# Another order of the score products in a cross-attention layer, with one mask moved ahead of one addition

## The chip, the cores and the metric

The kernel runs on one core of one Trainium2 chip, in one launch. The time is the device time of that core in microseconds (us); a kernel is run several times and the median counts. Five engines work side by side: PE multiplies matrices (its weight loads are listed apart as PEld), DVE is VectorE, ACT is ScalarE, POOL is GpSimd, and SP issues most of the transfers.

## The reference

One cross-attention layer with a feed-forward part, over 128 sequences of 128 tokens of width 256, 16 heads of 16 columns, hidden width 1024, all in float32:

```python
q = (query @ Wq + bq).reshape(b, s, N_HEADS, D_K).transpose(0, 2, 1, 3)
k = (key @ Wk + bk).reshape(b, s, N_HEADS, D_K).transpose(0, 2, 1, 3)
v = (values @ Wv + bv).reshape(b, s, N_HEADS, D_K).transpose(0, 2, 1, 3)
scores = jnp.einsum('bhqd,bhkd->bhqk', q, k) / jnp.sqrt(jnp.float32(D_K))
allowed = j < i + mask                      # mask = 0
scores = jnp.where(allowed, scores, NEG_INF)
attn = jax.nn.softmax(scores, axis=-1)
attn = attn.at[:, :, 0, :].set(0.0)
ctx = jnp.einsum('bhqk,bhkd->bhqd', attn, v)
attn_out = ctx.transpose(0, 2, 1, 3).reshape(b, s, d) @ Wo + bo
x = layer_norm(query + attn_out, ln1_g, ln1_b)
ffn = jax.nn.relu(x @ W1 + b1) @ W2 + b2
out = layer_norm(x + ffn, ln2_g, ln2_b)
```

`query` is `x`; `key` and `values` are both the context input. A query attends only to keys that stand before it.

## The kernel before

The 128 sequences are worked through as 64 pairs. The pairs run through a software pipeline: one step of it does the scores of pair p, the attention output of pair p-2, the first feed-forward product of pair p-3, the second of p-4, the projections of p+1, and so on. What each engine does, and in which order, is written out by hand: `ORDER` is a list of names, `step(p)`, for p from 9 to 60, calls the operation behind each name in turn, and every engine executes its own instructions in the order in which they were recorded. Pairs 7, 8, 61 and 62 use the same names, called one by one in lists of their own; the first seven pairs and the last are written out by hand. Semaphore waits between engines are put in by the framework where two operations touch the same data or the same bank.

PE's results go to eight banks, of 512 float32 numbers per partition. The operations around the change share them so:

- `weigh` (L586, L596) multiplies the attention weights of pair p-2 with its values; its result lies in bank 7.
- `context` (L614, two instructions on DVE) reads bank 7 and scales it by the softmax sums.
- `scores` (`scores_both`, L440) makes the scores of pair p. Its products use only 32 rows and 64 columns of the array, so that the array serves as eight tiles: four strips of 32 rows (r = 0 to 3) by the two sequences of the pair (s = 0, 1). The "high" half, queries 64 to 127, needs all 128 keys and takes products of 256 columns (two heads); its results lie in bank r. The "low" half, queries 0 to 63, can only see the first 64 keys and takes products of 128 columns; its results lie in bank 4+r. Each tile makes two low and two high products (m = 0 and 1). Strips 0 and 1 are called `one`, strips 2 and 3 `two`. So the low products of `two` write banks 6 and 7, and those of strip 3 write the bank that `context` reads.
- `maskA0`, `maskA1` (L464, DVE) add the mask to the low scores of strips 0 and 1 out of banks 4 and 5; `maskB` (L456) does so for strips 2 and 3, banks 6 and 7. `add3` (L1562) adds the mask to the high scores of strip 3 in bank 3, and `max3` (L1568) takes their maxima.
- `v1` (L1153, the values of pair p, bank 4) is the first work on PE behind the scores. `o1` (bank 5) and `q1` (bank 7) follow. These are products on the full array.

In the trace each float32 product shows as two records, a weight load and a matmul each; a score block of 32 products has 64.

Of the kernel before, what the change touches and what calls it, by code (L numbers as in the profile page):

```python
# [19 lines left out]
def tile_cross_attention_block(  # L20
# [83 lines left out]
    def weight(w, name):  # L104
        n = w.shape[0] // P
        t = const.tile([P, n, w.shape[1]], F32, tag=name, name=name)
        nc.sync.dma_start(t, w.rearrange("(k p) n -> p k n", p=P))
        return t
# [24 lines left out]
    wk = const.tile([P, KC, D], F32, tag="wk", name="wk")  # L133
# [29 lines left out]
    w1 = weight(W1, "w1")  # L163
# [3 lines left out]
    w2 = weight(W2, "w2")  # L167
# [18 lines left out]
    one = const.tile([1, P], F32, tag="one", name="one")  # L186
# [61 lines left out]
    def at_bank(i, name):  # L248
        return banks[:, i]
# [141 lines left out]
    def room(p, hi):  # L391

        st = states[p]
        if "sm" not in st:
            st["sm"] = wide(f"sm_{p}") if p != 1 else turned_all
        at = H * P if not hi else 0
        n = P if hi else HP
        st["sm", hi] = st["sm"][:, at : at + H * n].rearrange("p (h j) -> p h j", j=n)
        st["nmx", hi] = small.tile([P, H], F32, tag=f"nmx{hi}", name=f"nmx{hi}_{p}")
# [22 lines left out]
    def scores_both(p):  # L422

        st = states[p]
        st["both"] = True
        for hi in range(2):
            st["sps", hi] = [
                at_bank(r if hi else 4 + r, f"pss{hi}_{p}_{r}") for r in range(NS)
            ]
            room(p, hi)  # L430
        one, two = (0, 1), (2, 3)
        for strips, hi, m in (
            (one, 0, 0), (two, 1, 0), (one, 0, 1), (two, 1, 1),
            (one, 1, 0), (one, 1, 1), (two, 0, 0), (two, 0, 1),
        ):
            n = P if hi else HP
            for s in range(2):
                for r in strips:
                    strip, first = slice(32 * r, 32 * r + 32), s * P
                    nc.tensor.matmul(  # L440
                        st["sps", hi][r][
                            s * HP : (s + 1) * HP, m * 2 * n : (m + 1) * 2 * n
                        ].rearrange("p (e j) -> p e j", e=2),
                        st["qT"][strip, m, first + hi * HP : first + hi * HP + HP],
                        st["kT"][strip, m, :, first : first + n],
                        start=True, stop=True,
                    )
# [1200 lines left out]
    def bring_part(p, n):  # L1648
# [3 lines left out]
    OPS = {  # L1652
        "weigh": lambda p: weigh(p - 2),
        "scores": lambda p: scores_both(p),
        "context": lambda p: context(p - 2, True),
        "deviations": lambda p: scales_of(p),
# [96 lines left out]
    for n in range(3):  # L1753
        OPS[f"turn{n}"] = lambda p, n=n: turn(p, n < 2, n % 2)

    ORDER = """
        weigh addbo re0-2 vr-1 hf-2 re2-2 re1-2 turnx-1 xc2-1 re3-2 context scores res0 ro3-2
        ro0-2 br1 maskA0 ro2-2 add3 oc0 ro1-2 v1 maskA1 oc2 maskB hs0-1 o1 max3 vk1 vk0 q1
        lowmax eh7 oc1 v2 br0 xs2-1 qk w1-1 hs1-1 ok eh6 tokc-1 w2-1 tokx vk2 el3 oc3 hs3-1 v3
        add1 el4 w5-1 max1 br3 el0 add2 o2 cc0 wk-1 eh3 k1 finish1-1 vb ok2 va eh2 q2 stats2 o3  # L1760
        cc2 kk w6-1 max2 cc1 el6 add0 hs2-1 br2 h1-1 vf el2 ob oa max0 w3-1 qk2 cc3 eh5 xs0-1
        q3 eh0 xs1-1 o4 wk2-1 k2 qa finish2-1 qb hk-1 w7-1 or stats1 kk2 eh4 k3 xc0 means h6-1
        load-1 store-1 eh1 wb-1 xs3-1 ka xc1 wa-1 el5 q4 kb h5-1 xc3 turn1 el1 deviations
        w4-1 hk2-1 turn0 el7 k4 h7-1 res1 hk5-1 turn2 kr h2-1 vs-1 ks ha-1 qr h3-1 ks2 loadx norm2
        hb-1 h4-1 recip norm1 wr-1 turni v4
    """.split()

    EMPTY = {'w1': 5, 'h1': 4, 'w2': 5, 'h2': 4, 'w3': 5, 'h3': 5, 'w4': 4, 'h4': 5, 'w5': 4, 'h5': 5, 'w6': 4, 'h6': 5, 'w7': 5, 'h7': 4, 'v1': 3, 'o1': 1, 'q1': 2, 'k1': 2, 'v2': 3, 'o2': 2, 'q2': 2, 'k2': 3, 'v3': 2, 'o3': 2, 'q3': 3, 'k3': 2, 'v4': 2, 'o4': 2, 'q4': 3, 'k4': 2}
# [269 lines left out]
    tokens(5, "c")  # L2038
    bring(3, nc.sync, LATE_FIRST[7:])
    scores_both(4)  # L2040
    mask(4, 0, A)
    mask(4, 1, A)
# [31 lines left out]
    spread_values(4)  # L2074
    stack_values(4)
    scores_both(5)
    tokens(6, "c")
    mask_high(5, 2, 2)
# [1024 lines left out]
```

## Time and profile before

| what | value |
|---|---|
| median of 3 runs | 1464.37 us (1463.9 to 1467.12) |
| the profiled execution | 1463.95 us |
| its span in the profile | 1462.1 us |
| busy: PE, PEld, DVE, ACT, POOL | 99%, 95%, 94%, 89%, 87% |
| granted clock of TensorE | 1.0 over the span |
| one step of the pipeline | 21.97 us |

The span runs from the first to the last instruction. Idle time of an engine is listed with what ended it. A timeline merges neighbouring instructions of one line into a row: the start, how long until the last of them ended, and their number; a row names only the first shape.

### The profile page before, as it was taken

What the parts mean: (1) busy time and instruction counts of PE and PEld (TensorE: products, weight loads), DVE (VectorE), ACT (ScalarE), POOL (GpSimd) and SP (SyncE); (2) the same over time, 40 slices, a digit from 0 to 9 for tenths busy, and PEclk for the clock granted to TensorE, in tenths of its full rate; (3) what the DMA queues carried; (4) which work ended last, traced back from release to release, by engine and by line L of the source; (5) the groups of instructions that cost most, each with busy time, mean ns of one, the idle gap of its engine ahead of it and who ended that gap; (6) DMA issues with size and microseconds to landing.
All of it is one profiled execution on the core that took longest, in us unless ns stands there. A gap on an engine that the chain in (4) does not pass through costs nothing.

```text
span 1462.1 us, 62019 instructions
## 1 busy us (share of the span) xinstructions
PE 1445.1 (99%) x20713; PEld 1389.5 (95%) x20713; DVE 1372.1 (94%) x3175; ACT 1302.0 (89%) x5559; POOL 1268.4 (87%) x1872
## 2 busy tenths in 40 slices
PE   9999899999999999999999999999999999999998
PEld 7788799999999999999999999999999999999998
DVE  6987999999999999999999999999999999999777
ACT  5659899999999999999999999999999999999763
POOL 5977898988988988988988988988988988988875
PEclk9999999999999999999999999999999999999999
DMA  8264766766766766766766766766766766765451
GB/s 206 70 143 105 178 158 150 161 160 154 161 160 152 162 158 155 161 159 154 161 155 158 161 155 158 162 162 149 164 154 157 164 152 157 166 158 127 117 131 51
DMA packets 367881, 220.34 MB, mean 151 GB/s; under 512 B 280032, under 2 KB 335584, under 8 KB 367584
## 3 DMA queue, kind: packets, MB, share of 16 engines
q1 hardware_dynamic: 365296, 214.27, 64.2%
q8 instruction: 187, 3.06, 1.0%
q10 hardware_dynamic: 2288, 2.11, 0.7%
q14 instruction: 110, 0.90, 0.2%
HBM read 55.06 MB, written 18.09 MB: 50 GB/s over the span
## 4 chain that ended last, share of the span: by engine, by line
PE 92%; DVE 3%; POOL 1%; ACT 1%; DMA 1%; issue 1%; SPq 0%; POOLq 0%; DVEq 0%; ACTq 0%
PE banks L1153 48%; PE banks L1364 24%; PE banks L440 6%; PE banks L596 4%; PE banks L586 2%; PE banks L875 1%; PE banks L1050 1%; PE banks L300 1%; PE banks L977 1%; ACT sm L937 1%; PE banks L635 1%; POOL sm L476 1%; DVE sm L464 1%; PE banks L1412 0%; PE banks L894 0%
## 5 line engine op out<-in xcount | busy, mean ns | idle before, releaser
L937 ACT ACTIVATE sm<-banks,nmx 128x128 f32<-128x128 f32 x944 | 338.9, 391 | 19.1 <-DVE nmx L1568 15.5
L937 ACT ACTIVATE sm<-sm,nmx 128x64 f32<-128x64 f32 x944 | 323.4, 378 | 0.3 <-DVE nmx L926 0.3
L533 DVE STREAM_TRANSPOSE turned<-sm 128x1024 f32<-128x1024 f32 x186 | 217.1, 1215 | 4.8 <-DMA brought<-turned 3.0
L937 ACT ACTIVATION_READ_ACCUMULATOR sm<-banks,nmx 128x1 f32 x944 | 218.9, 232 | 0.0
L937 ACT ACTIVATION_READ_ACCUMULATOR sm<-sm,nmx 128x1 f32 x944 | 216.4, 229 | 0.0
L1153 PE MATMUL banks<-wt,hS 128*128 128x128 f32 x1344 | 177.7, 275 | 0.0
L1364 PE MATMUL banks<-xS,w1t 128*128 128x128 f32 x1344 | 177.4, 275 | 0.0
L1153 PEld LDWEIGHTS banks<-wt,hS 128*128 128x128 f32 x1344 | 163.6, 192 | 0.1
L1364 PEld LDWEIGHTS banks<-xS,w1t 128*128 128x128 f32 x1344 | 163.5, 192 | 0.1
L1568 DVE TENSOR_REDUCE nmx<-banks 128x4 f32<-128x512 f32 x224 | 152.6, 681 | 1.9
L1557 POOL TENSOR_TENSOR hS<-hT 128x512 f32<-128x512 f32 x116 | 147.8, 1275 | 3.1 <-ACT hT L882 1.4
L1364 PE MATMUL banks<-brought,w 128*128 128x128 f32 x896 | 118.3, 275 | 0.0
L1153 PE MATMUL banks<-w,hT 128*128 128x128 f32 x896 | 109.7, 275 | 0.0
L1364 PEld LDWEIGHTS banks<-brought,w 128*128 128x128 f32 x896 | 109.0, 192 | 0.0
L1618 POOL TENSOR_TENSOR x1b<-x,g_r 128x512 f32<-128x512 f32 x56 | 72.4, 1292 | 39.6 <-ACT x L709 39.6
L1153 PEld LDWEIGHTS banks<-w,hT 128*128 128x128 f32 x896 | 104.8, 192 | 0.0
L440 PE MATMUL banks<-kT,qT 32*64 32x128 f32 (+1 forms) x3840 | 98.4, 331 | 1.8 <-ACT vz L1278 1.5
L1393 ACT ACTIVATE hT<-hT,b1e_c 128x256 f32<-128x256 f32 x224 | 95.6, 509 | 0.3 <-DVE hT L1389 0.2
L1562 DVE TENSOR_TENSOR banks<-banks,neg 128x256 f32<-128x256 f32 x224 | 93.4, 417 | 0.1
L440 PEld LDWEIGHTS banks<-kT,qT 32*64 32x64 f32 x3840 | 79.5, 131 | 12.6 <-ACT vz L1278 1.8
L1219 ACT ACTIVATE kr<-banks,b_c 128x128 f32<-128x128 f32 x224 | 81.8, 403 | 2.7 <-PE banks L1153 2.7
L764 POOL TENSOR_TENSOR t<-t,g_r 128x512 f32<-128x512 f32 x62 | 79.1, 1276 | 5.3 <-ACT t L746 3.9
(324 smaller groups left out, 4795.9 us busy)
## 6 DMA issues: line engine op xcount, KB each, us to landing
brought<-turned SPq DMA_DIRECT2D x936, 128.0 KB, 2.4
out_dram<-t SPq DMA_DIRECT2D x63, 256.0 KB, 4.0
xb<-in_x_dram SPq DMA_DIRECT2D x124, 128.0 KB, 3.3
cb<-in_ctx_dram SPq DMA_DIRECT2D x124, 128.0 KB, 3.3
x<-in_x_dram SPq DMA_DIRECT2D x56, 256.0 KB, 2.9
kT<-kr SPq DMA_DIRECT2D x112, 128.0 KB, 2.2
brought<-turned SPq DMA_DIRECT2D x40, 96.0 KB, 2.5
w<-in_L_xattn_W_dram SPq DMA_DIRECT2D x2, 1024.0 KB, 7.4
```

What stands on the lines that cost most here:

```text
L440: nc.tensor.matmul(st["sps", hi][r][s * HP : (s + 1) * HP, m * 2 * n : (m + 1) * 2 * n].rearrange("p (e j) -> p e j", e=2), st["qT"][strip ...
L533: nc.vector.transpose(turned[:, :, at : at + 256].rearrange("p j (n a) -> p n j a", a=32), states[p]["sm", hi].rearrange("p h j -> p (h j) ...
L764: nc.gpsimd.tensor_tensor(t2, t2, g2_r[:, None, :].to_broadcast([P, 2, D]), ALU.mult)
L937: nc.scalar.activation(sm[:, h, :], src, AF.Exp, bias=nmx[:, h : h + 1], scale=1.0, **({"accum_out": st["su"][:, at : at + 1]} if summed e ...
L1153: nc.tensor.matmul(out, left(k) if self.depth > 1 else left, right(k) if self.depth > 1 else right, start=(n == 1 and k == 0), stop=(k == ...
L1219: nc.scalar.activation(self.k[:, m, s * P : (s + 1) * P], src, AF.Identity, bias=bk_c[:, m : m + 1], scale=1.0,)
L1364: nc.tensor.matmul(ps[:, i * P : (i + 1) * P].rearrange("p (n a) -> p n a", a=32), left(i), right, start=(n in (1, 2, 5) and i == 0), stop ...
L1393: nc.scalar.activation(self.hT[:, f, at], self.hT[:, f, at] if src is None else src, AF.Relu, bias=b1e_c[:, f : f + 1], scale=1.0,)
L1557: engine.tensor_tensor(c[:, n], left, right, how)
L1562: nc.vector.tensor_tensor(ps[:, :, HP:], ps[:, :, HP:], neg[:, 1, None, :].to_broadcast([P, 4, HP]), ALU.add)
L1568: nc.vector.tensor_reduce(states[p]["nmx", 1][:, 4 * b : 4 * b + 4], banks[:, b].rearrange("p (n j) -> p n j", j=P), AX.X, ALU.max, negate ...
L1618: nc.gpsimd.tensor_tensor(st["x1b"], st["x1b"] if n else st["x1"], (be1b_r if n else g1_r)[:, None, :].to_broadcast([P, 2, D]), ALU.add if ...
```

## The change

The order of the eight groups of four products in `scores_both` is another one, and in `ORDER` the names `maskA1` and `add3` change places. The rest of the list is only wrapped in other places; no instruction is added, removed or resized.

```diff
         for strips, hi, m in (
-            (one, 0, 0), (two, 1, 0), (one, 0, 1), (two, 1, 1),
-            (one, 1, 0), (one, 1, 1), (two, 0, 0), (two, 0, 1),
+            (one, 0, 0), (two, 1, 0), (one, 0, 1), (one, 1, 0),
+            (two, 0, 0), (two, 0, 1), (one, 1, 1), (two, 1, 1),
         ):
...
     ORDER = """
...
-        ro0-2 br1 maskA0 ro2-2 add3 oc0 ro1-2 v1 maskA1 oc2 maskB hs0-1 o1 max3 vk1 vk0 q1
...
+        ro3-2 ro0-2 br1 maskA0 ro2-2 maskA1 oc0 ro1-2 v1 add3 oc2 maskB hs0-1 o1 max3 vk1
```

Each group is (strips, 1 for high and 0 for low, m), and holds four products: two strips by two sequences.

On PE, one step before (a score block and the first product of `v1`; `64x128` is a low product, `64x256` a high one; a row stands for one instruction or, with xN, for N like it; the names in brackets are the engines and transfer queues whose semaphores it waits for):

```order
L440 MATMUL banks<-kT_171,qT_12548 64x128 [waits DMAHW4_49,DMAHW3_49,Activation_49]
L440 MATMUL banks<-kT_171,qT_12548 64x128 x3
L440 MATMUL banks<-kT_171,qT_12548 64x256 [waits DVE_49]
L440 MATMUL banks<-kT_171,qT_12548 64x256 x3
L440 MATMUL banks<-kT_171,qT_12548 64x128 x4
L440 MATMUL banks<-kT_171,qT_12548 64x256 x4
L440 MATMUL banks<-kT_171,qT_12548 64x256 [waits Activation_49]
L440 MATMUL banks<-kT_171,qT_12548 64x256 x7
L440 MATMUL banks<-kT_171,qT_12548 64x128
L440 MATMUL banks<-kT_171,qT_12548 64x128 [waits DVE_49]
L440 MATMUL banks<-kT_171,qT_12548 64x128 x6
L1153 MATMUL banks<-wv,cT_12586 128x128 [waits DVE_49]
```

The same step with the change:

```order
L440 MATMUL banks<-kT_171,qT_12548 64x128 [waits DMAHW4_49,DMAHW3_49,Activation_49]
L440 MATMUL banks<-kT_171,qT_12548 64x128 x3
L440 MATMUL banks<-kT_171,qT_12548 64x256 [waits DVE_49]
L440 MATMUL banks<-kT_171,qT_12548 64x256 x3
L440 MATMUL banks<-kT_171,qT_12548 64x128 x4
L440 MATMUL banks<-kT_171,qT_12548 64x256 [waits Activation_49]
L440 MATMUL banks<-kT_171,qT_12548 64x256 x3
L440 MATMUL banks<-kT_171,qT_12548 64x128
L440 MATMUL banks<-kT_171,qT_12548 64x128 [waits DVE_49]
L440 MATMUL banks<-kT_171,qT_12548 64x128 x6
L440 MATMUL banks<-kT_171,qT_12548 64x256 x8
L1153 MATMUL banks<-wv,cT_12586 128x128 [waits DVE_49]
```

The low product that waits for DVE (the first of strip 3) stood behind all sixteen high products and is now behind eight of them; eight high products stand behind it.

On DVE, the same place before:

```order
L614 TENSOR_TENSOR cxT<-banks,brought 128x8x32 [waits PE_49]
L614 TENSOR_TENSOR cxT<-banks,brought 128x8x32
L464 TENSOR_TENSOR sm_13386<-banks,neg 128x256 [waits PE_49,Activation_49]
L1562 TENSOR_TENSOR banks<-banks,neg 128x4x64 [waits PE_49]
L464 TENSOR_TENSOR sm_13386<-banks,neg 128x256
L456 TENSOR_TENSOR sm_13386<-banks,neg 128x512 [waits PE_49]
```

And with the change:

```order
L614 TENSOR_TENSOR cxT<-banks,brought 128x8x32 [waits PE_49]
L614 TENSOR_TENSOR cxT<-banks,brought 128x8x32
L464 TENSOR_TENSOR sm_13386<-banks,neg 128x256 [waits PE_49,Activation_49]
L464 TENSOR_TENSOR sm_13386<-banks,neg 128x256 [waits PE_49]
L1562 TENSOR_TENSOR banks<-banks,neg 128x4x64 [waits PE_49]
L456 TENSOR_TENSOR sm_13386<-banks,neg 128x512
```

`context` and `maskA0` keep their places; the second L464 (`maskA1`) and L1562 (`add3`) have changed theirs, and the wait for PE ahead of `maskB` is now the one ahead of `add3`. ACT, POOL and SP have the same instructions in the same order as before.

More of the change, by code (lines that the diff above doesn't have):

```diff
@@ L1756, in tile_cross_attention_block @@
     ORDER = """
-        weigh addbo re0-2 vr-1 hf-2 re2-2 re1-2 turnx-1 xc2-1 re3-2 context scores res0 ro3-2
-        ro0-2 br1 maskA0 ro2-2 add3 oc0 ro1-2 v1 maskA1 oc2 maskB hs0-1 o1 max3 vk1 vk0 q1
[L1759 to L1765, printed above, removed]
+        weigh addbo re0-2 vr-1 hf-2 re2-2 re1-2 turnx-1 xc2-1 re3-2 context scores res0
+        ro3-2 ro0-2 br1 maskA0 ro2-2 maskA1 oc0 ro1-2 v1 add3 oc2 maskB hs0-1 o1 max3 vk1
+        vk0 q1 lowmax eh7 oc1 v2 br0 xs2-1 qk w1-1 hs1-1 ok eh6 tokc-1 w2-1 tokx vk2 el3 oc3
+        hs3-1 v3 add1 el4 w5-1 max1 br3 el0 add2 o2 cc0 wk-1 eh3 k1 finish1-1 vb ok2 va eh2
+        q2 stats2 o3 cc2 kk w6-1 max2 cc1 el6 add0 hs2-1 br2 h1-1 vf el2 ob oa max0 w3-1 qk2
+        cc3 eh5 xs0-1 q3 eh0 xs1-1 o4 wk2-1 k2 qa finish2-1 qb hk-1 w7-1 or stats1 kk2 eh4
+        k3 xc0 means h6-1 load-1 store-1 eh1 wb-1 xs3-1 ka xc1 wa-1 el5 q4 kb h5-1 xc3 turn1
+        el1 deviations w4-1 hk2-1 turn0 el7 k4 h7-1 res1 hk5-1 turn2 kr h2-1 vs-1 ks ha-1 qr
+        h3-1 ks2 loadx norm2 hb-1 h4-1 recip norm1 wr-1 turni v4
     """.split()
```

## The prediction

> **What bounds the kernel now.** I read the page's head and its chain of waits first, then one step of the pipeline, then the score blocks.
>
> ```profile
> span 1462.1 us, 62019 instructions
> PE 1445.1 (99%) x20713; PEld 1389.5 (95%) x20713; DVE 1372.1 (94%) x3175; ACT 1302.0 (89%) x5559; POOL 1268.4 (87%) x1872
> PE 92%; DVE 3%; POOL 1%; ACT 1%; DMA 1%; issue 1%; SPq 0%; POOLq 0%; DVEq 0%; ACTq 0%
> ```
>
> PE is the bound: it holds 92% of the chain. The waits that PE still shows in the pipeline are of one kind only (busy time by engine over one step, then waits by who waited, for whom, us in total, times, longest):
>
> ```profile
> 734.09:756.06 21.97, 21.97 (x335) 21.54 (x329) 21.30 (x52) 20.83 (x93) 19.66 (x30) 1.00 0.69 158
> PEld banks L1153 <- DVE sm L464: 9.1, 52, 0.3
> DVE t L1299 <- PE banks L1153: 31.4, 60, 1.3
> ```
>
> So a step lasts as long as PE's work, at full clock, and the one regular gap is ahead of `v1`, 52 times 0.17 us, put down to `maskA0`. DVE has 0.67 us of air in a step (21.97 - 21.30), and spends some 0.5 of it (31.4/60) waiting for PE at one place. Whatever lengthens the stretch from `weigh` to `v1` on PE therefore lengthens the step one to one. The timeline of that stretch, about pair 34:
>
> ```profile
> 733.53 0.63 PE L596 MATMUL banks<-brought,vz 128*32 128x64 f32 x32
> 733.57 0.70 DVE L1624 STREAM_TRANSPOSE turned<-x 128x512 f32<-128x512 f32 x1
> 734.09 1.61 PE L440 MATMUL banks<-kT,qT 32*64 32x128 f32 x64
> 734.23 0.76 DVE L614 TENSOR_TENSOR cxT<-banks,brought 128x256 f32<-128x256 f32 x2
> 734.97 0.42 DVE L464 TENSOR_TENSOR sm<-banks,neg 128x256 f32<-128x256 f32 x1
> 735.31 0.42 DVE L1562 TENSOR_TENSOR banks<-banks,neg 128x256 f32<-128x256 f32 x1
> 735.63 0.52 PEld L1153 LDWEIGHTS banks<-wv,cT 128*128 128x128 f32 x4 [0.17 <-DVE sm L464]
> 735.64 0.41 DVE L464 TENSOR_TENSOR sm<-banks,neg 128x256 f32<-128x256 f32 x1
> 735.97 0.68 DVE L456 TENSOR_TENSOR sm<-banks,neg 128x512 f32<-128x512 f32 x1
> 736.57 0.68 DVE L1568 TENSOR_REDUCE nmx<-banks 128x4 f32<-128x512 f32 x1
> 736.96 0.41 PEld L1153 LDWEIGHTS banks<-xT,wq 128*128 128x128 f32 x3
> ```
>
> `weigh` ends at 734.16; `context` starts 0.07 later, which is as soon as it can, and ends at 734.99. Counted from the start of the scores (734.09) that is +0.90. `v1` loads at +1.54. `maskA0` is over at 735.39, 0.24 ahead of `v1`, so I doubt the releaser that is named. Three blocks in which `context` ran late decide it (start of the scores, `context`, load of `v1`):
>
> ```profile
> 184.61 1.59 PEld L440 LDWEIGHTS banks<-kT,qT 32*64 32x64 f32 x64
> 185.02 0.71 DVE L614 TENSOR_TENSOR cxT<-banks,brought 128x256 f32<-128x256 f32 x2
> 186.38 0.52 PEld L1153 LDWEIGHTS banks<-wv,cT 128*128 128x128 f32 x4 [0.17 <-issue]
> ...
> 1173.51 1.40 PEld L440 LDWEIGHTS banks<-kT,qT 32*64 32x64 f32 x64
> 1173.71 0.72 DVE L614 TENSOR_TENSOR cxT<-banks,brought 128x256 f32<-128x256 f32 x2
> 1175.08 0.41 PEld L1153 LDWEIGHTS banks<-wv,cT 128*128 128x128 f32 x3 [0.17 <-issue]
> ...
> 1349.56 1.44 PEld L440 LDWEIGHTS banks<-kT,qT 32*64 32x64 f32 x64
> 1349.81 0.72 DVE L614 TENSOR_TENSOR cxT<-banks,brought 128x256 f32<-128x256 f32 x2
> 1351.17 0.52 PEld L1153 LDWEIGHTS banks<-wv,cT 128*128 128x128 f32 x4 [0.17 <-issue]
> ```
>
> The end of `context` lies at +1.12, +0.92 and +0.97 there, the load of `v1` at +1.77, +1.57 and +1.61. In all four blocks `v1` loads 0.64 to 0.65 us behind the end of `context`, whatever else varies. What hangs between them is the low products of strips `two`: strip 3 must not write bank 7 before `context` has read it. **The release of bank 7 by `context`, and what the array still has to do behind it, sets the start of `v1`.** At present that is four records per tile (two low products). The records of L440 that run in two narrow windows, with their shapes, show that the array is full up to that moment:
>
> ```profile
> L440 PE MATMUL banks<-kT,qT x16: 374/374/412, 734.6 to 735.0; 32*64 32x256 f32 x16
> ...
> L440 PE MATMUL banks<-kT,qT x15: 267/374/374, 734.8 to 735.1; 32*64 32x256 f32 x11, 32*64 32x128 f32 x4
> ```
>
> In 734.96 to 735.03 only high records run, on every tile; in 735.02 to 735.06 four low ones have started, just as `context` (734.99) lets them. The old order has its high products of `two` cover the wait for `context` almost exactly.
>
> **The change part by part.** Nothing is added or removed: the same 64 records, 54 score blocks from 184.61 to 1349.56 that follow a `context` directly. What a record costs its tile (groups by form; then a row of the timeline):
>
> ```profile
> L440 PE MATMUL banks<-kT,qT 32*64 32x256 f32 x1920 | 93.8, 383 | 0.3 <-ACT vd L379 0.3
> L440 PE MATMUL banks<-kT,qT 32*64 32x128 f32 x1920 | 80.9, 279 | 1.5 <-ACT vz L1278 1.5
> 724.48 1.06 PE L1153 MATMUL banks<-wt,hS 128*128 128x128 f32 x8
> ```
>
> Eight records of 128 columns take 1.06 us where one lasts 0.275: (1.06 - 0.275)/7 = 0.112 us of array each. One of 256 columns lasts 383 - 279 = 104 ns more: 0.216.
>
> *The low products of `two`, moved ahead.* Tiles `two` have, ahead of the wait, two high products now (4 x 0.216 = 0.86, from +0.03 to about +0.95 with the first load) and one with the change (0.43, to about +0.51). From +0.51 to +0.95 they stand still: bank 7 comes free no sooner, since `context` starts when `weigh` ends. Behind the waiting product PE's queue holds the rest of the block, the last high products of `one` and `two`; `one` still has its first high product to finish (to about +0.92) and loses little.
>
> *The high products, moved to the end.* Behind the release the tiles of `two` now do two low and one high product instead of two low ones: two records of 256 columns more, 2 x 0.216 = 0.43 us. `one` needs 0.43 behind the release and is done earlier. The gap from the end of `context` to `v1` grows from 0.64 to 1.07, the block from +1.54 to +1.97. Bounds: not under 0.40 (0.05 off, should the first low load be ready in time); not over 0.53 (strict order, below). I take 0.43, for these are the same records on the same tiles one behind the other.
>
> *`maskA1` ahead of `add3`.* `maskA1` comes 0.33 us earlier (735.31 for 735.64) and frees bank 5, for which nobody waits: nothing. `add3` needs the high products of strip 3, now the last of all. The scores end 0.07 behind `v1`'s load (734.09 + 1.61 = 735.70), so at about +2.04, `add3` starts 0.07 later at +2.11 instead of +1.22; between `maskA1` (over at about +1.6) and there DVE is idle for 0.5. `maskB` and `max3` behind it come at +2.44 and +3.04 (were +1.88 and +2.48): 0.56 later, against 0.43 on PE, thus 0.13 behind. Who waits for them: `q1` needs `maskB` out of bank 7. `maskB` would end at +3.12, `q1` loads at +2.87 + 0.43 = +3.30: 0.18 of room, with a wake of 0.07 still enough. The exponentials on ACT wait for `max3` and fall 0.13 behind too; ACT has 1.14 us of air in a step (21.97 - 20.83). DVE makes the 0.13 good where it waits 0.5 for PE. I cost this part at nothing; the cover that hides it is that 0.18, and if it is gone the step pays the difference, up to 0.13.
>
> *The blocks outside.* Pair 5's block is written out by hand, and its mask of two high banks stands ahead of the masks that PE waits for:
>
> ```profile
> 105.57 0.70 DVE L917 TENSOR_TENSOR banks<-banks,neg 128x512 f32<-128x512 f32 x1 [0.24 <-PE banks L440]
> 105.72 0.63 PEld L440 LDWEIGHTS banks<-kT,qT 32*64 32x64 f32 x30 [0.77 <-ACT vd L379]
> 107.91 0.30 PEld L300 LDWEIGHTS banks<-xT,wq 128*128 128x128 f32 x2 [1.56 <-DVE sm L464]
> ```
>
> The mask would start behind the moved high products: 105.72 + two low (0.45) + one high (0.43) + the record's tail and wake, about 0.23 = 106.85, so 1.3 us later, and L300 behind it as well. Pairs 4, 6 and 7 can lose 0.43 each in the same way as the others; pairs 8 and 63 nothing, as `context` was done long before or is not there. That makes 0 to 2.6; since PE has other waits there that can swallow some of it, I take half, 1.3.
>
> **The sum.** 54 x 0.43 + 1.3 = 24.5 us. The profiled execution took 1463.95 us (span 1462.1 and 1.85 around it), 0.4 under the median of the runs shown; 1463.95 + 24.5 = 1488.5, as a median 1489.
>
> **The rivals.**
>
> *Strict order.* If all score products must start in program order, the last high product of `one` begins only with the last low record of `two`, and that of `two` only behind the first record of `one`. The last low record starts at 0.95 + 0.05 + 3 x 0.112 = +1.34; then 0.216 for `one`, 2 x 0.216 for `two`, and the 0.09 that lie now between the end of the low records (0.95 + 0.05 + 4 x 0.112 = +1.45) and the load of `v1` (+1.54): +2.07, 0.53 a step, 54 x 0.53 + 1.3 = 29.9, or 1494. Against it: records of 256 columns start behind the first low ones now, though they precede them in the program:
>
> ```profile
> L440 PE MATMUL banks<-kT,qT x19: 267/268/375, 735.0 to 735.4; 32*64 32x128 f32 x12, 32*64 32x256 f32 x7
> ```
>
> In 735.40 to 735.44 seven records of 256 columns run; none lasts over 375 ns, so they began after 735.02, and the later ones after the first four low ones. [...]
>
> *A second wait.* The 0.13 us by which DVE and ACT fall behind meets too little room, at `q1` or at a later product behind an exponential: up to 0.13 a step more, 7 us, 1489 to 1496. For it: the room of 0.18 is small. Against it: the 0.5 of DVE's wait.
>
> *Faster.* If bank 7 came free early enough, every tile would end with equal work and without the late first load: 4 x 0.112 + 4 x 0.216 + 0.05 = 1.36 for the products, less by about 0.09 than now, 54 x 0.09 = 4.9, or 1459.5. It decides from a `context` that ends before about +0.45. The rows have it at +0.90 and it cannot start before `weigh` has ended, at +0.07, and takes 0.76; so this needs the wait to belong to something else.
>
> *Little or no change.* The stall might be paid by another wait that shrinks. PE has none but the 0.17 at `v1`, which is the change of shape and stays (184.61 and 1349.56 show it without `maskA0`).
>
> **How the numbers follow.** Forecast, 0.40 to 0.46 a step: 0.75, its own range 1486 to 1492. Strict order 0.06, second wait 0.10; a smaller loss (part of the stall hidden, 1470 to 1484) 0.03; faster 0.04; no change 0.02. The range of 1483 to 1496 leaves out the last three and the outer edge of the second wait. A difference under 0.2% (2.9 us) counts as none here: faster 0.04, the same 0.02, slower 0.94.
>
> **What would show it.** A step of 22.40 us; `context` still ending at about +0.90 and `v1` loading near +1.97, 1.07 behind it; the high records last in the block; a pause in which only a tile or so of `two` works, from +0.5 to +0.95; `add3` waiting for the score products for 0.5, `q1` not waiting. It would be wrong if `v1` loaded at +1.45 (the wait was not `context`'s), if the gap behind `context` were not 1.07, or if a wait of PE appeared at `q1`.

## The result, and the profile after

The changed kernel takes 1492.95 us (median of 5 runs, 1490.04 to 1493.81) and the kernel before 1466.16 us (5 runs, 1463.9 to 1467.39): a ratio of 1.0183, with a 95% interval of 1.0167 to 1.0198. It is slower by 26.8 us. The forecast was 24.5 us more, 1489 us, in a range of 1483 to 1496.

The head of the page and the chain of waits of the changed kernel (its profiled execution took 1493.81 us):

```profile
span 1492.0 us, 62014 instructions
PE 1472.4 (99%) x20713; PEld 1389.3 (93%) x20713; DVE 1376.0 (92%) x3175; ACT 1298.5 (87%) x5559; POOL 1270.8 (85%) x1872
PE 94%; DVE 2%; ACT 1%; POOL 1%; DMA 1%; issue 1%; SPq 0%; POOLq 0%; DVEq 0%; ACTq 0%
```

PE is still the bound, and it is "busy" for 27.3 us more (1472.4 - 1445.1) with the same 20713 instructions. Nothing was added, so this is for the most part time in which some tile of the array works while others stand still; stretches of half clock, below, have a part in it. PEld shows it: its busy time did not change (1389.3 for 1389.5), so on balance the 29.9 us of the longer span are time without a weight load. Which waits they are stands in the list of waits of the changed kernel (who waited, for whom: us in total, times, longest):

```profile
DVE banks L1562 <- PE banks L440: 26.1, 54, 1.0
PEld banks L1153 <- DVE sm L464: 20.8, 54, 0.4
PEld banks L440 <- DVE cxT L614: 16.3, 54, 0.3
```

All three occur 54 times, once in each score block of the pipeline. The third is new by name: the score products wait for `context` in the middle of the block. The first is `add3` waiting for the last high products. Two more rows of the same list bear on what was forecast of the masks:

```profile
DVE t L1299 <- PE banks L1153: 31.4, 60, 1.3
ACT sm L937 <- DVE nmx L1568: 22.9, 55, 2.6
```

The first stands in the list of the kernel before with the same figures; the second, the exponentials waiting for `max3`, was 15.5 us there. The block about pair 34 in the timeline of the changed kernel (start, duration, engine, line):

```profile
705.20 0.63 PE L596 MATMUL banks<-brought,vz 128*32 128x64 f32 x32
...
705.76 0.65 PEld L440 LDWEIGHTS banks<-kT,qT 32*64 32x64 f32 x34
705.76 2.04 PE L440 MATMUL banks<-kT,qT 32*64 32x128 f32 x64
705.89 0.76 DVE L614 TENSOR_TENSOR cxT<-banks,brought 128x256 f32<-128x256 f32 x2
...
706.63 0.76 DVE L464 TENSOR_TENSOR sm<-banks,neg 128x256 f32<-128x256 f32 x2
706.70 0.64 PEld L440 LDWEIGHTS banks<-kT,qT 32*64 32x64 f32 x30 [0.30 <-DVE cxT L614]
...
707.72 0.52 PEld L1153 LDWEIGHTS banks<-wv,cT 128*128 128x128 f32 x4 [0.39 <-DVE sm L464]
...
707.85 0.43 DVE L1562 TENSOR_TENSOR banks<-banks,neg 128x256 f32<-128x256 f32 x1 [0.47 <-PE banks L440]
...
708.19 0.68 DVE L456 TENSOR_TENSOR sm<-banks,neg 128x512 f32<-128x512 f32 x1
...
709.06 0.53 PEld L1153 LDWEIGHTS banks<-xT,wq 128*128 128x128 f32 x4
```

The weight loads of L440 now come in two rows, 34 and 30, with 0.30 of nothing between them that `context` (L614) ends. From the block's start at 705.76, `context` ends at +0.89, the second row starts at +0.94, `v1` (the first L1153) loads at +1.96 and `add3` (L1562) starts at +2.09. `q1` (the last row) loads at +3.30 without a wait, 0.19 behind the end of `maskB` (L456, 708.87). A step, in the table of busy times by window:

```profile
705.76:728.16 22.40, 22.40 (x335) 21.50 (x329) 21.37 (x52) 20.75 (x93) 19.71 (x31) 1.00 0.69 155
```

It lasts 22.40 us for 21.97 before, at full granted clock. By the unrounded times `v1` loads 1.073 to 1.074 us behind the end of `context` in all 54 blocks (before: 0.642 to 0.645).

**Where the 29.9 us of the spans lie.** The starts of the score blocks in the two timelines divide the difference (1492.0 - 1462.1) into four parts:

| stretch | before | after | more |
|---|---|---|---|
| up to the block of pair 4 (the instructions there are the same) | 85.29 | 86.88 | 1.59 |
| block of pair 4 to block of pair 9 | 99.32 | 103.39 | 4.07 |
| 54 blocks of the pipeline: 53 steps to the block of pair 62, and that block's own 0.43 | | | 22.79 + 0.43 = 23.22 |
| the rest | | | 1.02 |

The first part is not the change's. The mean granted clock from 20 to 40 us was 0.93 (the table of windows of the changed kernel, third number from the end), where the profiled execution of the kernel before had full clock over its span:

```profile
20.00:40.00 20.00, 20.00 (x241) 16.46 (x241) 17.99 (x28) 15.36 (x30) 19.18 (x11) 0.93 0.86 189
```

Experiment 7, which runs the old order at that place, shows 0.94 there and starts pair 4's block 1.33 later than the kernel before. So this differs from run to run. The second is pair 5 above all; from block to block it is 0.43 more behind pair 4's, 3.01 behind pair 5's, 0.43 less behind pair 6's, 1.04 more behind pair 7's, and nothing behind pair 8's. Pair 5's block, DVE's mask (L917) and PE's next load (L300), in the timeline of the changed kernel, and then the table of windows just behind (the third number from the end is the granted clock):

```profile
106.31 0.62 PEld L440 LDWEIGHTS banks<-kT,qT 32*64 32x64 f32 x26 [0.33 <-ACT cxT L628]
...
109.22 0.70 DVE L917 TENSOR_TENSOR banks<-banks,neg 128x512 f32<-128x512 f32 x1 [2.08 <-PE banks L440]
...
111.56 0.50 PEld L300 LDWEIGHTS banks<-xT,wq 128*128 128x128 f32 x2 [2.93 <-DVE sm L464]
```

```profile
111.40:114.80 3.40, 3.24 (x8) 2.62 (x9) 3.33 (x7) 3.40 (x21) 0.00 (x0) 0.50 0.61 145
114.80:118.20 3.40, 3.40 (x17) 3.00 (x16) 2.21 (x6) 3.40 (x21) 0.00 (x0) 1.00 0.41 96
```

The block of pair 5 starts at 106.31; L917 stands at +2.91 (before: 105.57 - 104.28 = +1.29), and L300 at +5.25 (before +3.63), 1.62 later. No weight load runs ahead of it for 2.93 us instead of 1.56 (no matmul for 2.48 instead of 1.10), and then PE has a clock of 0.50 for 3.4 us. The matching window of the kernel before, behind its own L300 at 107.91, has the full clock:

```profile
107.90:111.30 3.40, 3.38 (x16) 3.00 (x17) 3.33 (x6) 3.40 (x22) 0.00 (x0) 1.00 0.68 160
```

From the block of pair 5 to that of pair 6 it takes 22.52 us for 19.51: 3.01, of which 1.62 is the longer wait; the other 1.4 is put down to the half clock. Experiment 6 (below) shows the half clock without the longer wait: L300 stands at +3.63 there, as in the kernel before, and from block to block it takes 21.00, which is 1.49 more.

The last part, 1.02, cannot be put down to the change. From the block of pair 62 to that of pair 63 it takes 36.28 in the kernel before and 37.56 in the changed one, but 36.86 in experiment 2, with the old order of products, and 36.52 in experiment 4, whose blocks last as long as those of the changed kernel.

### The profile page after: what moved, and what is told of

Read it like the earlier page. It is cut to its first block, busy times and chain, and to the rows that moved or that the text cites. A ratio compares the mean times of both kernels' runs of the same rounds, so it can differ in the third digit from the quotient of the medians.

```text
span 1492.0 us, 62014 instructions
## 1 busy us (share of the span) xinstructions
PE 1472.4 (99%) x20713; PEld 1389.3 (93%) x20713; DVE 1376.0 (92%) x3175; ACT 1298.5 (87%) x5559; POOL 1270.8 (85%) x1872
## 3 DMA queue, kind: packets, MB, share of 16 engines
q8 instruction: 187, 3.06, 0.9%
q10 hardware_dynamic: 2288, 2.11, 0.7%
## 4 chain that ended last, share of the span: by engine, by line
PE 94%; DVE 2%; ACT 1%; POOL 1%; DMA 1%; issue 1%; SPq 0%; POOLq 0%; DVEq 0%; ACTq 0%
PE banks L1153 47%; PE banks L1364 23%; PE banks L440 8%; PE banks L596 4%; PE banks L586 2%; PE banks L875 2%; PE banks L300 2%; PE banks L977 2%; PE banks L1050 1%; PE banks L635 1%; ACT sm L937 1%; PE banks L356 1%; DVE sm L464 1%; PE banks L1412 0%; PE banks L894 0%
## 5 line engine op out<-in xcount | busy, mean ns | idle before, releaser
L937 ACT ACTIVATE sm<-banks,nmx 128x128 f32<-128x128 f32 x944 | 342.8, 406 | 28.6 <-DVE nmx L1568 22.9
L937 ACT ACTIVATE sm<-sm,nmx 128x64 f32<-128x64 f32 x944 | 329.9, 398 | 0.2 <-DVE nmx L926 0.2
L937 ACT ACTIVATION_READ_ACCUMULATOR sm<-sm,nmx 128x1 f32 x944 | 234.9, 249 | 0.0
L937 ACT ACTIVATION_READ_ACCUMULATOR sm<-banks,nmx 128x1 f32 x944 | 231.4, 245 | 0.0
L533 DVE STREAM_TRANSPOSE turned<-sm 128x1024 f32<-128x1024 f32 x186 | 220.1, 1226 | 3.5 <-ACT sm L937 1.8
L1153 PE MATMUL banks<-wt,hS 128*128 128x128 f32 x1344 | 177.6, 275 | 0.0
L1153 PEld LDWEIGHTS banks<-wt,hS 128*128 128x128 f32 x1344 | 163.6, 192 | 0.1
L440 PE MATMUL banks<-kT,qT 32*64 32x128 f32 (+1 forms) x3840 | 122.6, 334 | 1.9 <-ACT vz L1278 1.5
L1562 DVE TENSOR_TENSOR banks<-banks,neg 128x256 f32<-128x256 f32 x224 | 94.1, 420 | 26.2 <-PE banks L440 26.1
L1153 PE MATMUL banks<-w,hT 128*128 128x128 f32 x896 | 109.7, 275 | 0.0
L1153 PEld LDWEIGHTS banks<-w,hT 128*128 128x128 f32 x896 | 104.8, 192 | 0.0
L440 PEld LDWEIGHTS banks<-kT,qT 32*64 32x64 f32 x3840 | 77.1, 131 | 26.7 <-DVE cxT L614 16.3
L1219 ACT ACTIVATE kr<-banks,b_c 128x128 f32<-128x128 f32 x224 | 88.4, 432 | 3.2 <-PE banks L1153 3.2
```

What stands on the lines that cost most here:

```text
L440: nc.tensor.matmul(st["sps", hi][r][s * HP : (s + 1) * HP, m * 2 * n : (m + 1) * 2 * n].rearrange("p (e j) -> p e j", e=2), st["qT"][strip ...
L533: nc.vector.transpose(turned[:, :, at : at + 256].rearrange("p j (n a) -> p n j a", a=32), states[p]["sm", hi].rearrange("p h j -> p (h j) ...
L937: nc.scalar.activation(sm[:, h, :], src, AF.Exp, bias=nmx[:, h : h + 1], scale=1.0, **({"accum_out": st["su"][:, at : at + 1]} if summed e ...
L1153: nc.tensor.matmul(out, left(k) if self.depth > 1 else left, right(k) if self.depth > 1 else right, start=(n == 1 and k == 0), stop=(k == ...
L1219: nc.scalar.activation(self.k[:, m, s * P : (s + 1) * P], src, AF.Identity, bias=bk_c[:, m : m + 1], scale=1.0,)
L1562: nc.vector.tensor_tensor(ps[:, :, HP:], ps[:, :, HP:], neg[:, 1, None, :].to_broadcast([P, 4, HP]), ALU.add)
```

## The experiments

**Experiment 1: the products' order alone.** The changed kernel with the old `ORDER`, so that `add3` stands ahead of `maskA1` again:

```diff
-        ro3-2 ro0-2 br1 maskA0 ro2-2 maskA1 oc0 ro1-2 v1 add3 oc2 maskB hs0-1 o1 max3 vk1
+        ro0-2 br1 maskA0 ro2-2 add3 oc0 ro1-2 v1 maskA1 oc2 maskB hs0-1 o1 max3 vk1 vk0 q1
```

> The new order of the score products, with the old place of add3 ahead of maskA1. Theory (context's release of bank 7 sets the block; add3 is held until the last high products): the block from the start of the scores to v1's load is again 1.97 us, add3 starts at +2.11, maskA1 behind it at +2.44 and over at +2.85; o1, which needs bank 5 and would load at +2.63, waits some 0.28 us. Step 22.40 + 0.28 = 22.68, in all some 15 us slower than the changed kernel, about 1508. Rival (the place of the mask on VectorE does not matter): step 22.40, 1493.

Measured: 1510.74 us, a ratio of 1.0308 (1.0293 to 1.0324) and a step of 22.73. Around pair 34, in the timeline of this kernel, whose block starts at 713.31:

```profile
715.27 0.52 PEld L1153 LDWEIGHTS banks<-wv,cT 128*128 128x128 f32 x4 [0.38 <-issue]
...
715.40 0.43 DVE L1562 TENSOR_TENSOR banks<-banks,neg 128x256 f32<-128x256 f32 x1 [0.80 <-PE banks L440]
...
715.75 0.41 DVE L464 TENSOR_TENSOR sm<-banks,neg 128x256 f32<-128x256 f32 x1
...
716.27 0.52 PEld L1153 LDWEIGHTS banks<-wo,cxT 128*128 128x128 f32 x4 [0.26 <-issue]
```

`v1` loads at +1.96 as in the changed kernel. But `maskA1` (L464) now stands behind `add3` and ends at 716.16, and `o1`, which writes bank 5, gets its load 0.11 behind that, after 0.26 of waiting. So the exchange of the two masks is worth 22.73 - 22.40 = 0.33 us a step, once the products are in the new order.

**Experiment 2: the masks' exchange alone.** The old order of the products with the new `ORDER`, the same line of the diff the other way round.

> The old order of the score products, with maskA1 ahead of add3. Theory: nobody waits for either within 0.2 us, so nothing moves: step 21.97, ratio to the kernel before 1.000 within 0.002, block 1.54. Rival (the exchange has a part in the loss, since add3 and max3 come 0.33 us later): max3 late by up to 0.33, step up to 22.1, about 1470.

Measured: 1464.94 us, a ratio of 0.9994 (0.9985 to 1.0003); step 21.97, `v1` at +1.54. The wait ahead of `v1` in the list of waits of this kernel:

```profile
PEld banks L1153 <- DVE sm L464: 9.2, 53, 0.3
```

It was 9.1 us over 52 times before. `add3` comes 0.33 later here, and the step does not move. The exchange costs nothing and gains nothing by itself; the loss belongs to the products.

**Experiment 3: a longer `context` in the kernel before.** The second of its two instructions is issued twice, with the same result; the order of the products is the old one:

```diff
-                for q in (1, 0):
+                for q in (1, 0, 0):
```

> The kernel before, but the second instruction of context is issued twice in the pipeline (the same result written once more), so that context ends some 0.34 us later. Theory (v1 hangs on context's end even in the old order): v1's load moves by the same 0.34, from +1.54 to +1.88, still 0.64 behind the end of context; step 22.31, 54 x 0.34 = 18 us slower, about 1483. Rival (v1 waits for maskA0, as the list of waits has it): maskA0 ends at 1.30 + 0.34 = +1.64, v1 loads at about +1.70, step 22.13, 54 x 0.16 = 9 us slower, about 1474.

Measured: 1491.3 us, a ratio of 1.0171 (1.0157 to 1.0185), step 22.43. The block in the timeline of this kernel:

```profile
704.92 2.07 PE L440 MATMUL banks<-kT,qT 32*64 32x128 f32 x64
705.06 1.22 DVE L614 TENSOR_TENSOR cxT<-banks,brought 128x256 f32<-128x256 f32 x3
...
706.33 0.42 PEld L440 LDWEIGHTS banks<-kT,qT 32*64 32x64 f32 x14 [0.29 <-DVE cxT L614]
...
706.91 0.52 PEld L1153 LDWEIGHTS banks<-wv,cT 128*128 128x128 f32 x4 [0.17 <-issue]
```

`context` ends at 706.28 and `v1` loads at 706.91. By the unrounded times that is +1.35 and +2.00, and `v1` is 0.64 behind, as in the four blocks of the prediction. The size was off: the repeat starts 0.03 behind the end of the instruction whose output it writes again, where the second instruction starts 0.08 ahead of the end of the first, and so it adds 0.46, not 0.34. The time follows `context` one to one, and the last 14 weight loads of L440, the low products of `two`, are what it holds. `maskA0` does not set it: it ends here at 706.60, 0.31 ahead of `v1`, for 0.24 in the kernel before, while the distance from `context` stays.

**Experiment 4: a block that ends in low products.** The changed kernel, with the last low group of `two` at the very end:

```diff
-            (two, 0, 0), (two, 0, 1), (one, 1, 1), (two, 1, 1),
+            (two, 0, 0), (one, 1, 1), (two, 1, 1), (two, 0, 1),
```

> The changed kernel, but the last group of low products of strips two goes to the very end, so that the block ends with products of 128 columns while the same two high records per tile stay behind the release. Theory (what lies behind the release counts, in whatever order): v1 loads at +1.97 as in the changed kernel, step 22.40, about 1493. Rival (the block's last product being one of 256 columns costs by itself, since the array drains longer before it changes shape): 0.11 us less a block, step 22.29, 6 us faster than the changed kernel, about 1487.

Measured: 1492.22 us, a ratio of 1.0183 (1.0169 to 1.0197), step 22.40. The timeline of this kernel, block start 704.99:

```profile
705.94 0.85 PEld L440 LDWEIGHTS banks<-kT,qT 32*64 32x64 f32 x30 [0.30 <-DVE cxT L614]
...
706.87 0.43 DVE L1562 TENSOR_TENSOR banks<-banks,neg 128x256 f32<-128x256 f32 x1 [0.25 <-PE banks L440]
706.96 0.52 PEld L1153 LDWEIGHTS banks<-wv,cT 128*128 128x128 f32 x4 [0.17 <-issue]
```

`v1` loads at +1.97 again. `add3` comes 0.21 earlier and the gap that is put down at `v1` shrinks from 0.39 to 0.17, yet the step stays. So it is not the product of 256 columns at the end that costs: what counts is how much work of a tile stands behind the release of bank 7, in whatever order.

**Experiments 5 and 6: no release at all.** `context` multiplies the softmax sums with themselves instead of reading bank 7, so that no product waits for it. This leaves the attention weighting out of the result. In 5 it is done to the changed kernel, in 6 to the kernel before:

```diff
-                        to[:, :, :, :, q], pc[:, :, :, :, q], inv[:, :, :, :, q], ALU.mult
+                        to[:, :, :, :, q], inv[:, :, :, :, q], inv[:, :, :, :, q], ALU.mult
```

> The changed kernel, but context in the pipeline multiplies the inverse sums by themselves instead of by bank 7 (same instructions and shapes on VectorE; the attention weighting is left out of the result), so that nothing holds bank 7 when the low products come. Theory: the tiles never stand still, each has 0.05 + 4 x 0.112 + 4 x 0.216 = 1.36 us of work, v1 loads at about +1.45, step 21.88: 54 x 0.52 = 28 us faster than the changed kernel, about 1465, and 0.09 a step under the kernel before; what the blocks ahead of pair 8 and the tail lose stays. Rival (the release of bank 7 is not what holds the block): step 22.40, 1493.

> The kernel before with the same edit of context (the attention weighting is left out of the result). Theory: the low products are no longer 0.05 us late with their first weights; v1 loads at +1.47 to +1.50, step 21.90 to 21.93, 2 to 4 us faster than the kernel before. Rival (the old order does not wait for context at all): step 21.97, the same time.

Measured in 5: 1481.09 us, a ratio of 1.0105 (1.009 to 1.0121), step 22.15, `v1` at +1.71. Measured in 6: 1465.18 us, a ratio of 1.0002 (0.9993 to 1.0011), step 21.96, `v1` at +1.52. The loads of the block and of `v1`, in the timeline of 5 and then of 6:

```profile
701.49 1.33 PEld L440 LDWEIGHTS banks<-kT,qT 32*64 32x64 f32 x64
...
703.21 0.52 PEld L1153 LDWEIGHTS banks<-wv,cT 128*128 128x128 f32 x4 [0.39 <-DVE sm L464]
```

```profile
690.74 1.35 PEld L440 LDWEIGHTS banks<-kT,qT 32*64 32x64 f32 x64
...
692.26 0.52 PEld L1153 LDWEIGHTS banks<-wv,cT 128*128 128x128 f32 x4 [0.17 <-DVE sm L464]
```

The pause in the middle of the loads is gone in 5 (64 in one row), and the step is 0.25 shorter. The theory had 0.52, for the new order should then take the 1.45 that equal work per tile gives. It does not. Without any wait the new order is still slower than the old one, by 22.15 - 21.96 = 0.19. And the old order gains only 0.01 from a free bank, where 0.04 to 0.07 were expected: its time is the one that the rival had. Experiment 3 shows that the old order does wait for `context` when that ends later. So in the kernel before two limits lie almost at the same place: the release puts `v1` at +1.54, and without the release something else puts it at +1.52 (experiment 8).

**Experiment 8: why the free order takes 1.71.** In experiment 5 the weight loads of the last high products of `two` come late. Here the last two groups of that kernel change places (the attention weighting is left out again):

```diff
-            (two, 0, 0), (two, 0, 1), (one, 1, 1), (two, 1, 1),
+            (two, 0, 0), (two, 0, 1), (two, 1, 1), (one, 1, 1),
```

> The free version of the changed kernel (context does not read bank 7, so the attention weighting is left out of the result), with the last two groups in the other order: the last high products of strips two come ahead of those of one. It asks why the free new order loads v1 at +1.71 and not at the +1.45 that equal work per tile would give. In the free run the loads of the last high products of two show late: one tile at +0.87, the other three at +1.112, +1.128 and +1.145, 0.1 to 0.16 behind the moment at which their low products leave the tile, and 0.011 behind the end of the second of one's first high products (+1.10). Theory A (PE hands out products in program order and only so far ahead; whichever products stand last are held until older ones end): now the last products of one are held in the same way, three loads at about +1.11, last record at about +1.38 to +1.41, v1 at about +1.69 to +1.72, step 22.13 to 22.16, 1480 to 1482 us. Theory B (it lies in strips two, in going from a low to a high product behind a full tile): two no longer waits behind one; its last records start at about +1.20, one's as now or earlier, v1 at about +1.46 to +1.50, step about 21.9, 1467 to 1469 us.

Measured: 1479.69 us, a ratio of 1.0099 (1.0081 to 1.0117), step 22.15, `v1` at +1.71. The end of the block in its timeline (block start 701.04):

```profile
702.67 0.43 DVE L1562 TENSOR_TENSOR banks<-banks,neg 128x256 f32<-128x256 f32 x1
702.75 0.52 PEld L1153 LDWEIGHTS banks<-wv,cT 128*128 128x128 f32 x4 [0.39 <-DVE sm L464]
```

`add3` comes 0.19 earlier than in 5 (+1.63 for +1.82), since `two` is done earlier, and `v1` does not move. The records of one block each, in us from its start (products numbered from 1 to 32 in program order):

```
kernel               product 16 ends   loads of products 30, 31, 32 start
5, `two` last        1.101             1.112  1.128  1.145
8, `one` last        1.098             1.110  1.126  1.143
6, old order         1.123             1.134  1.151  1.167
```

Whichever products stand at places 30 to 32, they are loaded from 0.011 to 0.012 behind the end of product 16, although in 5 their tiles should be ready earlier: the last low records of these tiles start at 0.863 to 0.898, and by the estimate of 0.112 us of array a record the next could start at 0.975 to 1.010; it does at 1.116 to 1.149. So in these kernels it is their place in the program that holds them, and not their tile: in experiment 5 product 29 is loaded at 0.87, while 13 to 16 still run, and 30 to 32 only behind the end of 16. What exactly they wait for, these rows do not settle: products 13 to 16 end within 0.02 of each other, so it may be any of them. In the old order low products stand in the last places, short ones, and the delay costs 1.52 - 1.45 = 0.07, if the 1.45 of the theory is what an undelayed block would take; in the new one a product of 256 columns per tile is delayed.

**Experiment 7: the old order outside the pipeline.** Pairs 4 to 8 and the last keep the old order of products:

```diff
+            (one, 0, 0), (two, 1, 0), (one, 0, 1), (two, 1, 1),
+            (one, 1, 0), (one, 1, 1), (two, 0, 0), (two, 0, 1),
+        ) if p < 9 or p == NP - 1 else (
             (one, 0, 0), (two, 1, 0), (one, 0, 1), (one, 1, 0),
```

> The changed kernel, but pairs 4 to 8 and pair 63 keep the old order of the products. Theory: the pipeline's 54 blocks cost 54 x 0.43 = 23.2 us and the tail 0.9, together 24: about 1490, 3 to 5 us under the changed kernel, because pair 5's stall of 2.9 us ahead of its next projection, and the half clock that follows it, are gone. Rival (the blocks ahead of the pipeline cost 1.3 at most, and the rest of the difference is run to run): 1 us under the changed kernel, about 1492.

Measured: 1488.6 us (1487.41 to 1489.07), a ratio of 1.0163 (1.0149 to 1.0176), 4.35 under the median of the changed kernel. By the two ratios it is 2.9, with intervals that overlap. Over its own runs of the kernel before (1464.96) it is 23.6 us, where the 54 blocks of the pipeline make 54 x 0.43 = 23.2. The window behind pair 5's L300, in the table of windows of this kernel:

```profile
109.20:113.00 3.80, 3.75 (x17) 3.34 (x18) 3.70 (x7) 3.80 (x24) 0.00 (x0) 1.00 0.58 138
```

The clock stays full, L300 starts at +3.63 of its block as in the kernel before, and from pair 5's block to pair 6's it takes 19.52. From pair 4's block to pair 9's it takes 99.37, as before (99.32). So the blocks by hand are the source of some 3 to 4 us.

## Why the prediction was right, and where it was off

- **What sets `v1`.** Right. The release of bank 7 by `context` was read from three late blocks against the releaser that the profile names, and experiment 3 shows it directly: `v1` moves with `context` one to one (0.64 behind it) where `maskA0` has long ended. The list of waits of the changed kernel still names `maskA0` at `v1`, for 20.8 us. What the prediction did not see is how close another limit lies: without the release the old order still takes +1.52 (experiment 6), so in the kernel before the release decides by 0.015 us only. And the gap of 0.17 ahead of `v1`, which was said to stay, grew to 0.39; with low products at the end it is 0.17 again (experiment 4) and `v1` stays where it was, so the gap goes with the products that stand last and costs nothing by itself.
- **Two high records more behind the release: 0.43 a step.** Right: 1.07 from the end of `context` to `v1` in all 54 blocks, `v1` at +1.97 where `context` is not late, the step 22.40. 54 x 0.43 = 23.2 of the 29.9 us.
- **The stall from +0.51 to +0.95.** Right: the weight loads pause until +0.94.
- **The masks.** `add3` was forecast at +2.11, `maskB` at +2.44 and `max3` at +3.04; they came at +2.09 to +2.10, +2.43 and +3.03. `q1` loads at +3.30 with 0.19 of room, so there is no second wait. The exponentials on ACT wait 0.13 longer for `max3` (22.9 us for 15.5, over 55 times), as forecast, and nothing on PE follows from it. DVE does make the 0.13 good, but not where the prediction had it: the wait at L1299 is 31.4 us over 60 times before and after, and by an earlier L1299, at +7.69 for +7.26, the lag is already down to 0.43. But "frees bank 5, for which nobody waits" was read from the old order only: had `maskA1` not been moved, `o1` would wait for it, 0.33 a step (experiment 1). A term of nothing was right because two parts of the change belong together.
- **The blocks outside: 1.3 forecast, some 3 to 4 measured.** This is the term that was mis-sized, and it makes up most of the distance to the result. The profiled executions have 4.07 there, and experiment 7 has 2.9 by the ratios and 4.35 by the medians. The forecast had L917 1.3 later in pair 5 (the terms it gives for that add up to 106.83, not 106.85) and L300 behind it, and halved that for other waits that might swallow it. Nothing swallowed it: both came 1.6 later, with a stretch of half clock behind, worth 1.4 to 1.5, which no term had; and pair 7 lost 1.04 where 0.43 was allowed for, which stays unexplained. The 1.59 before pair 4 is the profiled execution's own and not a cost of the change; with the 1.02 behind pair 62 it is part of why the spans differ by 29.9 and the medians by 26.8.
- **Strict order (1494).** Its figure lay nearest to the measured time, and the range of the second wait (1489 to 1496) held it too, but neither by its mechanism: there is no second wait, and strict order needs `v1` at +2.07, 1.17 behind `context`, and a step of 22.50. That all score products start in program order was an assumption that no run shows; the trace has 1.07 behind `context` in all 54 blocks and speaks against it for products on different tiles.
- **Faster (1459.5).** Its condition was not met, and its size was wrong too. With the condition met (experiment 5) the new order takes 1.71 and not 1.45, because the loads of the last products come late (experiment 8). There was nothing to win here even with a free bank.

## What to carry to other kernels

Where a product waits for a bank, count for each array tile the work that stands behind the release: here that work, and not the total, set the end (`v1` loads 0.64 us behind `context` with two low products of a tile behind the release, 1.07 with two low and one high), and the longer products were best placed ahead of it, as cover. When the releaser that a profile names had ended long before, look for blocks in which another candidate ran late, and see which distance stays fixed. Cost the blocks that are written by hand outside the loop one by one, and ask of each longer idle time of PE whether the clock falls behind it, as it did here to 0.50 for 3.4 us behind 2.93 us without a weight load.

## What the runs showed that was not expected

**The clock behind an idle PE.** Ahead of pair 5's L300 no weight load ran for 2.75 to 2.93 us (no matmul for 2.3 to 2.5) in the five runs that had the new order there (the changed kernel and experiments 1, 4, 5 and 8). In the changed kernel 3.4 us at a clock of 0.50 followed, and the eight loads of L300 took 3.06. In experiment 8 the mean clock was 0.84 from 111.20 to 114.50 and 0.67 from 114.60 to 118.00. Experiments 1 and 4 have slow loads there, 1.78 for five and 2.20 for six; for experiment 5 no fall of the clock is shown, its first two loads took 0.30 as in the kernel before. With the old order there no weight load ran for 1.56 us in five kernels (before and experiments 2, 3, 6 and 7). The eight loads then took 1.59 in four of them and 2.76 in experiment 6, where the clock fell, in its table of windows:

```profile
107.60:111.00 3.40, 3.40 (x10) 2.68 (x9) 3.30 (x6) 3.40 (x21) 0.00 (x0) 0.50 0.69 163
```

So the length of the idle time does not decide alone: behind the same 1.56 us the clock fell to 0.50 in one of five. What decides at 1.56 us was not tried.

**How far ahead PE goes.** That the last weight loads are held by their place in the program was seen in the three kernels whose `context` leaves bank 7 alone (experiments 5, 6 and 8, the loads of products 30 to 32 starting from 0.011 to 0.012 us behind the end of product 16). Whether the limit is a count of products, of instructions, or something else that happens to fall there was not tried.
